# Edge beats paced by TensorE's traced pieces, and the last tile's output product moved into the second tile period

## The chip, the core and the metric

The kernel runs on one core of a Trainium2 chip. The metric is the device time of one execution in microseconds; three runs are shown for the kernel before. A core has TensorE (matrix products into PSUM), VectorE, ScalarE, GpSimd and SyncE, each working through its own queue in order. The profile writes PE, DVE, ACT, POOL and SP for them, and PEld for TensorE's weight loads. DMAs are issued from the queues of SP, ACT and POOL.

## The reference

625 nodes with 1024 features and 10000 directed edges go through two layers.

```
xn = layernorm(x)
x  = x + GAT(xn, edges) + linear_attention(xn)      # 4-head graph attention; 16 heads, phi = elu + 1
x  = x + bit_ffn(layernorm(x))                      # int8 activations, ternary weights
xn = layernorm(x)
x  = x + SAGE(xn, edges) + linear_attention(xn)
x  = x + attention_and_experts(x)                   # dense attention, 8 experts, 2 per token
```

The change lies in the first layer. Its graph attention computes for every edge, and for a loop at each node, `e = att . leaky_relu(xl[src] + xr[dst])` for four heads, takes the softmax over the edges that end in one node, and sums `xl[src]` with these weights. The result goes through `W_up`. The linear attention computes `q`, `k`, `v` by three 1024 x 1024 products, and its result goes through the output weights `Wo`. Both are added to `x`.

## The kernel before

The 625 nodes are five tiles of 125. The first part of the kernel, up to about 640 us, computes the whole first layer and begins the second. Its order is written out by hand: `do(prep, pe, after, after2)` (class `Stream`, L174) emits a piece of TensorE work, after emitting the drains (`after`) of the pieces before it. Each engine runs what was emitted for it, in that order.

**The edge stage.** The 10000 edges lie in 79 columns of up to 128. Column `t` needs two gathers from DRAM (`ga`, rows of `xl` by source; `gb`, rows of `xr` by destination, L591), a score on VectorE (L599, L571, L572, L574), an exponential on ScalarE (L578) and a scatter of four values into a table in DRAM (L609). Gathers and scatters are indirect DMAs issued by GpSimd, 237 in all. Columns go in groups of two (40 groups, the last with one short column); `ga` and `gb` have four buffers each. One *beat* `g` (`one_beat`, L662) emits the gathers of group `g`, the scores of group `g - 3`, the exponentials of `g - 4` and the scatters of `g - 5` (the list `lags`), and in beats 1 to 5 also the loop scores of one node tile. From the output products on, `lags` is 1, 1, 2, and a beat may emit four scatters.

Beats are laid between the pieces of the linear attention by an estimate: every piece calls `work(us)` with the time that it is held to take (L681), and a beat is emitted whenever the sum reaches 8.2 us times the number of beats so far. The pieces: for each half of the columns and each tile a `key` and a `value` product (20 in all) with up to six `count` pieces after each (79; L447, fed by one-hot tiles that VectorE writes up to eight ahead); eight `states`; eight `query` and eight `answer` pieces; then the output products `mixed(t)` with `Wo` (L717), 16 products of 512 columns each.

**The output products.** `mixed(0)` begins before the last answer with six of eight row blocks. Then come `mixed(3)` and `mixed(4)`, whose results VectorE drains with the bias into the tile `kept`; `weight_sums` (L740: absolute sums of the three FFN weight matrices on VectorE, L742), a small product `pm` with their means (L744), the rest of `mixed(0)`, `mixed(1)`, `mixed(2)`, and the rounding of the FFN weights to three values (`ternary`, L755). Tiles 0 to 2 stay in PSUM, which has three double banks for them. Beats that are left over are emitted after that.

**The tile periods.** `load_table(t)` (L803) fetches a tile of the table (`tb`), from GpSimd's queue. For each tile, `weigh` (L817) multiplies it with edge counts, `sums` makes the sums (`pg`) and `turn_sums` transposes them, `up_again` (L872) adds the product with `W_up` to the bank that holds `mixed(t)`, or for tiles 3 and 4 to a new bank, and adds that to `x` (L885). `x` itself is loaded again by GpSimd after the first table tile, and `bo` or `kept` is added to it (L1051). One period later the FFN of that tile follows (`ptr`, `pgu`, `phT`, `pdn`), and one later still its rows are transposed for layer 2. From period 2 on, `spacer()` puts the first `key` and `value` products of layer 2 between; their weights are asked for by `lin1.weights(0)`, and take the buffers of `Wo`.

Of the kernel before, what the change touches and what calls it, by code (L numbers as in the profile page):

```python
# [14 lines left out]
ALU = mybir.AluOpType  # L15
# [6 lines left out]
P = 125  # L22
# [8 lines left out]
KC = D // 128  # L31
# [22 lines left out]
def attempt(ctx: ExitStack, tc: tile.TileContext, w: dict, out: bass.AP, shifted: bool):  # L54

    nc = tc.nc
# [105 lines left out]
    def rows_dma(eng, dst, src):  # L162

        eng.dma_start(out=dst[0:112], in_=src[0:112])
        eng.dma_start(out=dst[112:P], in_=src[112:P])
# [42 lines left out]
    hold = {}  # L208

    def mid(shape, name):  # L210
        return midp.tile(shape, FP, tag="mid", name=name)
# [4 lines left out]
    class LinearAttention:  # L216
# [26 lines left out]
        def key(self, t):  # L243
            kf, bk, wk = self.kf, self.bk, self.wk

            def pe():
                hold["pk", t] = ps1("pk")
                group(hold["pk", t][:P], [(self.xnT[:, k, nodes(t)], wk(k)) for k in range(KC)])

            def after():  # L250
                kb = mix.tile([P, 512], FP, tag="kb", name="kb", bufs=1)
                nc.vector.tensor_tensor(kb, hold.pop(("pk", t))[:P], bk[:P], op=ALU.add)
                ke = mix.tile([P, 512], FP, tag="ke", name="ke", bufs=1)
                nc.scalar.activation(ke, kb, AF.Exp)
                nc.scalar.activation(kb, kb, AF.Relu)
                hold["k", t] = ke, kb

            def after2():
                ke, kb = hold.pop(("k", t))
                nc.vector.scalar_tensor_tensor(kf[:, t, :], ke, 1.0, kb, op0=ALU.min, op1=ALU.add)  # L260

            do(None, pe, after, after2)
            self.work(4.8)

        def value(self, t):
            v, bv, wv = self.v, self.bv, self.wv

            def pe():
                hold["pv", t] = ps1("pv")
                group(hold["pv", t][:P], [(self.xnT[:, k, nodes(t)], wv(k)) for k in range(KC)])  # L270

            def after():
                nc.vector.tensor_tensor(v[:, t, :, 0:128],
                                        hold.pop(("pv", t))[:P].rearrange("p (a b) -> p a b", a=4),
                                        bv[:P].rearrange("p (a b) -> p a b", a=4), op=ALU.add)

            do(None, pe, after)
            self.work(4.8)

        def states(self):  # L280

# [44 lines left out]
        def answer(self, m, oT):  # L326
            kv, a = self.kv[m // 4], m % 4

            def pe():
                hold["pdo"] = [feat("pd", [(kv[:, a, 128:256], hold["qf", m])]),  # L330
                               feat("po", [(kv[:, a, 0:128], hold["qf", m])])]

            def after():
                pd, po = hold["pdo"]
                z = mix.tile([128, NP], FP, tag="qe", name="z", bufs=1)
                nc.vector.tensor_scalar(halves(z), pd, 1e-6, None, op0=ALU.add)
                nc.vector.reciprocal(z, z)
                nc.vector.tensor_tensor(halves(oT[:, m, :]), po, halves(z), op=ALU.mult)

            do(None, pe, after)  # L340
            self.work(2.7)

    with ExitStack() as st0:
        main = st0.enter_context(tc.tile_pool(name="l0", bufs=1))
# [7 lines left out]
        with ExitStack() as edges:  # L352
# [327 lines left out]

            def work(us):  # L681
                beat["us"] += us
                while beat["us"] >= 8.2 * beat["g"] and chunks:
                    one_beat()

            work(0.0)
# [1 line left out]
            for c in range(2):  # L688
                if c:
                    lin.half(c)  # L690
                for t in range(NT):
                    for f in (lin.key, lin.value):
                        f(t)
                        part["held"] = max(part["held"] - 1, 0)
                        for _ in range(6):
                            if count():
                                work(0.72)
                states.append(lin.states())
                if c == 0:
                    for f in states[0]:  # L700
                        f()
# [12 lines left out]
                f()  # L714


            def mixed(t, ks=range(KC), keep=None):  # L717
                for c in range(2):
                    def pe(c=c):
                        if c == 0 and ks[0] == 0:  # L720
                            hold["px", t] = ps2("px1")
                        for k in ks:
                            nc.tensor.matmul(hold["px", t][:P, c, :], lhsT=oT[:, k, nodes(t)], rhs=wo[c](k),
                                             start=(k == 0), stop=(k == KC - 1 and keep is not None))

                    def after():
                        px = hold.pop(("px", t))
                        for c in range(2):
                            nc.vector.tensor_tensor(keep[:, c, :], px[:P, c, :], bo[c][:P], op=ALU.add)

                    do(None, pe, after if keep is not None and c == 1 else None)
                    work(0.6 * len(ks))

            dn = main.tile([128, 2, D], BF, name="dn")
            part3 = main.tile([128, 3], FP, name="part3")
# [43 lines left out]
            gu = wpool.tile([128, KC, 512], BF, tag="w", name="gu", padded_shape=[128, KC, 512])  # L779
            made = [gu[:, :, 0:256], gu[:, :, 256:512], dn]  # L780
            lags[:] = 1, 1, 2
            kept = mid([P, 2, 2, 512], "kept")
            mixed(3, keep=kept[:, 0])
            weight_sums()
            mixed(4, keep=kept[:, 1])
            weight_means()
            mixed(0, range(6, KC))
            for t in (1, 2):
                mixed(t)
                ternary(t)  # L790
# [9 lines left out]
        late = st0.enter_context(tc.tile_pool(name="l0r", bufs=1, reuse_waits="tile"))  # L800


        def load_table(t):  # L803

            hold["tb", t] = mid([P, NT, P, 4], "tb")
            if not shifted:
                rows_dma(nc.gpsimd, hold["tb", t].rearrange("p s d h -> p s (d h)"),
                         tview[:, :, t * 4 * P:(t + 1) * 4 * P])

        def weigh(t):  # L810
# [59 lines left out]
            do(None, pe, after)  # L870

        def up_again(t):  # L872
            kept_apart = t >= 3
            px = ps2("px1") if kept_apart else hold.pop(("px", t))

            def pe():
                goT = hold.pop(("goT", t))
                for c in range(2):
                    for k in range(2):
                        nc.tensor.matmul(px[:P, c, :], lhsT=goT[:, k, :],  # L880
                                         rhs=wu[:, k, c * 512:(c + 1) * 512],
                                         start=(kept_apart and k == 0), stop=(k == 1))

            def after():
                nc.vector.tensor_tensor(x[:, t, :].rearrange("p (c n) -> p c n", c=2), px[:P],  # L885
                                        x[:, t, :].rearrange("p (c n) -> p c n", c=2), op=ALU.add)

            do(None, pe, after)
# [116 lines left out]
            return p1, f1, f2, f3, f4, p5, f5  # L1005


        load_table(0)
        for t in range(NT):
            rows_dma(nc.gpsimd, x[:, t, :], xrows[t])  # L1010
        load_table(1)
# [4 lines left out]
        def spacer():  # L1016

            f, t = next(kv_pieces)
            getattr(lin1, f)(t)

        for p in range(NT + 2):
            do()
            if p >= 2:
                made_of[p - 2][5]()
            if 1 <= p <= NT:
                made_of[p - 1] = ffn(p - 1)
                made_of[p - 1][0]()
            if p >= 3:
                spacer()
            if p >= 2:  # L1030
                made_of[p - 2][6]()
            if p == 0:
                xnT1 = bigT("xnT1")
                nc.gpsimd.memset(xnT1[:, :, N:NP], 0.0)
                lin1 = LinearAttention(xnT1, ("L1_Wq", "L1_Wk", "L1_bk", "L1_Wv", "L1_bv"), w["L1_bq"],
                                       lambda us: None, nc.gpsimd)
            if p < NT:
                sums(p)
            if 1 <= p <= NT:
                made_of[p - 1][1]()  # L1040
                do()
                made_of[p - 1][2]()
            do()
            if p + 1 < NT:
                weigh(p + 1)
            if p + 2 < NT:
                load_table(p + 2)
            for t in ((0, 1), (2, 3, 4))[p] if p < 2 else ():
                for c in range(2):
                    xc = x[:, t, c * 512:(c + 1) * 512]  # L1050
                    nc.vector.tensor_tensor(xc, xc, bo[c][:P] if t < 3 else kept[:, t - 3, c, :], op=ALU.add)  # L1051
            if p == 0:
                lin1.weights(0)
            if p == 1:
                lin1.half(0, loaded=True)
            if 2 <= p <= NT:
                spacer()
            if p < NT:
                turn_sums(p)
            if 1 <= p <= NT:  # L1060
                made_of[p - 1][3]()
            do()
            if p < NT:
                up_again(p)
            if 1 <= p <= NT:
                made_of[p - 1][4]()
# [621 lines left out]
    for i in range(3):  # L1688
        d = 1 << i
# [240 lines left out]
```

## Time and profile before

| | us |
|---|---|
| median of three runs | 2255.76 (2247.72 to 2260.8) |
| the profiled execution | 2253.51 |
| its span in the trace | 2251.8 |
| TensorE busy | 2115.4 |
| VectorE busy | 715.1 |
| GpSimd busy | 341.6 |
| mean granted TensorE clock | 0.973 |

The span is what the trace covers; all sums below are made in it. The clock is the share of full speed that was granted to TensorE. Beginnings of stages in the trace: first key piece 49.0 us, first gather 56.3, end of the last output product 402.5, first product of the tile periods 456.3, layer 2's first key piece 524.1.

### The profile page before, as it was taken

To read this page: it belongs to the slowest core of one execution; us is meant where nothing else is said; L and a number is where in the kernel's file an instruction comes from. 1 tells how busy PE (TensorE), PEld (TensorE's weight loads), DVE (VectorE), ACT (ScalarE), POOL (GpSimd) and SP (SyncE) were. 2 spreads that over 40 slices of the span, in tenths; PEclk is the share of its full clock that TensorE was granted. 3 is DMA by queue.
4 is the path that set the end of the run, shared out by engine and by line. 5 is a ranking of instruction groups with operands and counts; after the bars stand their busy time and mean duration, and the time that the engine had idled before them with its cause. 6 is when DMAs were issued, how large, how long until landed. Compare 5 with 4: busy or idle time off the path is not lost. (4 is left out here: it accounts for less than half of the span.)

```text
span 2251.8 us, 17353 instructions
## 1 busy us (share of the span) xinstructions
PE 2115.4 (94%) x6934; PEld 1211.3 (54%) x6934; DVE 715.1 (32%) x1216; ACT 194.6 (9%) x354; POOL 341.6 (15%) x351
## 2 busy tenths in 40 slices
PE   7999999158899989999999999999999999999998
PEld 5665664035444658764445776556754444444443
DVE  4855486365621482001013233322111111111112
ACT  2101110001110110000000011110000000000000
POOL 1566477610000040010000000110000000000010
PEclk9999999668999999999999999999999999999999
DMA  8352332350030210231212111030288997898742
GB/s 278 118 165 70 136 127 55 120 135 23 19 103 29 84 56 1 75 116 61 75 38 103 38 38 38 19 102 7 87 313 323 332 331 283 321 332 303 262 149 94
DMA packets 145848, 301.62 MB, mean 134 GB/s; under 512 B 12370, under 2 KB 22436, under 8 KB 145754
## 3 DMA queue, kind: packets, MB, share of 16 engines
q1 hardware_dynamic: 123412, 243.18, 30.4%
q0 software_dynamic: 17664, 47.47, 7.1%
q10 hardware_dynamic: 4678, 9.72, 1.4%
q8 instruction: 58, 0.95, 0.2%
q14 instruction: 36, 0.29, 0.0%
HBM read 277.49 MB, written 22.84 MB: 133 GB/s over the span
## 5 line engine op out<-in xcount | busy, mean ns | idle before, releaser
L130 PE MATMUL pu<-w,xgT 128*128 128x512 f32 x768 | 333.9, 593 | 1.9 <-DVE xgT L1224 1.9
L130 PEld LDWEIGHTS pu<-w,xgT 128*128 128x128 f32 x768 | 144.0, 190 | 174.8 <-issue 172.0
L130 PE MATMUL pyb<-w,hb 128*128 128x512 f32 x384 | 174.3, 598 | 2.4 <-ACT yb L105 2.1
L130 PE MATMUL pv<-w,xnT 128*125 128x512 f32 x320 | 142.6, 599 | 4.7 <-DVE x L985 4.7
L130 PE MATMUL pk<-w,xnT 128*125 128x512 f32 x320 | 140.6, 592 | 0.0
L130 PE MATMUL pq<-xnT,w 128*128 128x313 f32 x512 | 138.1, 428 | 2.0 <-ACT qf L319 1.2
L130 PE MATMUL p<-tT,w 128*128 128x313 f32 x512 | 136.3, 428 | 0.4 <-DVE tT L1224 0.4
L130 PEld LDWEIGHTS pq<-xnT,w 128*128 128x128 f32 x512 | 96.5, 190 | 42.1 <-ACT qf L319 3.7
L130 PEld LDWEIGHTS pyb<-w,hb 128*128 128x128 f32 x384 | 69.8, 189 | 90.9 <-issue 74.8
L130 PEld LDWEIGHTS p<-tT,w 128*128 128x128 f32 x512 | 96.8, 190 | 37.9 <-issue 1.2
L1764 DVE TENSOR_TENSOR su<-pu,su 128x512 f32<-128x512 f32 x24 | 16.6, 692 | 314.2 <-ACT su L1763 314.2
L130 PEld LDWEIGHTS pv<-w,xnT 128*125 128x125 f32 x320 | 59.9, 190 | 78.9 <-issue 72.2
L130 PEld LDWEIGHTS pk<-w,xnT 128*125 128x125 f32 x320 | 59.6, 188 | 71.6 <-issue 70.7
L609 POOL DMA_INDIRECT table<-es,at x79 | 83.3, 1054 | 60.7 <-issue 32.8
L1747 POOL DMA_INDIRECT xg<-rows_d,slots x12 | 11.4, 947 | 524.7 <-PE pxg L1754 449.0
L591 POOL DMA_INDIRECT ga<-xl_d,si x79 | 79.9, 1012 | 62.7 <-DVE es L574 22.9
L130 PE MATMUL pg<-xl,pT 125*125 125x65 f32 x200 | 32.2, 332 | 57.5 <-DVE pT L817 55.4
L591 POOL DMA_INDIRECT gb<-xr_d,di x79 | 81.6, 1032 | 25.2 <-issue 25.2
L130 PE MATMUL px<-w,hT 128*125 128x512 f32 x160 | 70.3, 592 | 0.0
L130 PE MATMUL px<-w,oT 128*125 128x512 f32 x160 | 70.3, 592 | 0.0
L130 PE MATMUL ph<-meanT,w 128*128 128x313 f32 x256 | 70.1, 426 | 0.0
L130 PE MATMUL ph<-xnT,w 128*128 128x313 f32 x256 | 70.0, 427 | 0.0
(368 smaller groups left out, 2507.2 us busy)
## 6 DMA issues: line engine op xcount, KB each, us to landing
w<-in_eW_dram SPq DMA_DIRECT2D x144, 1024.0 KB
w<-in_L_Wk_dram SPq DMA_DIRECT2D x8, 1024.0 KB
w<-in_L_Wv_dram SPq DMA_DIRECT2D x8, 1024.0 KB
w<-in_L_Wq_dram SPq DMA_DIRECT2D x8, 1024.0 KB
w<-in_L_Wo_dram SPq DMA_DIRECT2D x8, 1024.0 KB
w<-in_W_self_dram SPq DMA_DIRECT2D x8, 1024.0 KB
w<-in_W_neigh_dram SPq DMA_DIRECT2D x8, 1024.0 KB
w<-in_sW_dram SPq DMA_DIRECT2D x8, 1024.0 KB
```

What stands on the lines that cost most here:

```text
L130: nc.tensor.matmul(dst, lhsT=lhsT, rhs=rhs, start=(i == 0), stop=(i == len(pairs) - 1))
L591: nc.gpsimd.indirect_dma_start(out=ab[g][side][0:p, j, :], out_offset=None, in_=src[:, :], in_offset=bass.IndirectOffsetOnAxis(ap=ix[0:p, ...
L609: nc.gpsimd.indirect_dma_start(out=table[:, :], out_offset=bass.IndirectOffsetOnAxis(ap=at[0:p, lo + j:lo + j + 1], axis=0), in_=es[0:p, l ...
L1747: nc.gpsimd.indirect_dma_start(out=xg, out_offset=None, in_=rows_d[:, :], in_offset=bass.IndirectOffsetOnAxis(ap=slots[:, b:b + 1], axis=0))
L1764: nc.vector.tensor_tensor(su, pu[:, 0, :], su, op=ALU.mult)
```

## The change

The estimates and due times of the beats are new, tile 4's output product is made in two halves in the second tile period, with layer 2's weights asked for after it, and the first table tile is loaded from ScalarE's queue.

```diff
 key, value:
-            self.work(4.8)
+            self.work(7.0)
 answer:
-            self.work(2.7)
+            self.work(2.3)
 one count:
-                                work(0.72)
+                                work(0.7)
 mixed, for each half:
-                    work(0.6 * len(ks))
+                    work(0.87 * len(ks))
 work:
-                while beat["us"] >= 8.2 * beat["g"] and chunks:
+                while beat["us"] >= 8.0 + 5.2 * min(beat["g"], 5) + 8.1 * max(beat["g"] - 5, 0) and chunks:
                     one_beat()

-            def mixed(t, ks=range(KC), keep=None):
-                for c in range(2):
+            def mixed(t, ks=range(KC), keep=None, cs=(0, 1)):
+                for c in cs:
...
-            kept = mid([P, 2, 2, 512], "kept")
-            mixed(3, keep=kept[:, 0])
+            kept = mid([P, 2, 512], "kept")
+            mixed(3, keep=kept)
             weight_sums()
-            mixed(4, keep=kept[:, 1])
+            mixed(0, range(6, KC))
             weight_means()
-            mixed(0, range(6, KC))
             for t in (1, 2):
                 mixed(t)
                 ternary(t)

-        def load_table(t):
+        def load_table(t, eng=nc.gpsimd):
...
-                rows_dma(nc.gpsimd, hold["tb", t]...
+                rows_dma(eng, hold["tb", t]...

 up_again:
-            kept_apart = t >= 3
+            kept_apart = t == 3

-        load_table(0)
+        load_table(0, nc.scalar)
         for t in range(NT):
             rows_dma(nc.gpsimd, x[:, t, :], xrows[t])
         load_table(1)
...
             if p >= 3:
                 spacer()
+            if p == 1:
+                mixed(4, cs=(0,))
...
-                    nc.vector.tensor_tensor(xc, xc, bo[c][:P] if t < 3 else kept[:, t - 3, c, :], op=ALU.add)
-            if p == 0:
+                    nc.vector.tensor_tensor(xc, xc, kept[:, c, :] if t == 3 else bo[c][:P], op=ALU.add)
+            if p == 1:
+                mixed(4, cs=(1,))
                 lin1.weights(0)
-            if p == 1:
                 lin1.half(0, loaded=True)
```

In the order of the changed kernel's instructions, TensorE's end of the edge stage reads: six blocks of tile 0, the last answer, tile 3, two blocks of tile 0, `pm`, tile 1, tile 2, and then the first `pg`. In the second period the first half of tile 4 stands between tile 0's up-product and tile 1's `pg`, the second half between tile 0's `pgu` and tile 1's transposes. All 43 beats come before the end of tile 2's product.

More of the change, by code (lines that the diff above doesn't have):

```diff
@@ L277, in value @@
             do(None, pe, after)
-            self.work(4.8)
+            self.work(7.0)
         def states(self):
@@ L800, in attempt @@
         late = st0.enter_context(tc.tile_pool(name="l0r", bufs=1, reuse_waits="tile"))
-        def load_table(t):
+        def load_table(t, eng=nc.gpsimd):
             hold["tb", t] = mid([P, NT, P, 4], "tb")
             if not shifted:
-                rows_dma(nc.gpsimd, hold["tb", t].rearrange("p s d h -> p s (d h)"),
+                rows_dma(eng, hold["tb", t].rearrange("p s d h -> p s (d h)"),
                          tview[:, :, t * 4 * P:(t + 1) * 4 * P])
```

## The prediction

> **What bounds the kernel now.** I read the slices first: TensorE is full everywhere except around 400 to 640 us. The stretches of that region, by engine (length, busy time and instruction count of PE, PEld, DVE, ACT, POOL, then granted clock, DMA share, GB/s):
>
> ```profile
> 375.00:402.50 27.50, 27.45 (x64) 11.66 (x63) 8.13 (x11) 0.42 (x2) 18.97 (x18) 1.00 0.42 137
> 402.50:445.20 42.70, 0.00 (x0) 0.00 (x0) 18.07 (x29) 1.04 (x5) 27.01 (x25) 0.56 0.24 77
> 445.20:456.30 11.10, 0.01 (x1) 0.01 (x1) 1.10 (x2) 0.00 (x0) 5.80 (x10) 0.50 0.73 174
> 456.30:480.00 23.70, 20.05 (x90) 15.68 (x90) 13.70 (x19) 1.66 (x2) 4.97 (x9) 0.67 0.73 185
> 510.00:524.00 14.00, 13.05 (x56) 11.59 (x57) 5.68 (x13) 2.47 (x4) 2.00 (x3) 0.52 0.20 51
> ```
>
> TensorE stands still for 54 us, and runs at half to two thirds of its clock for 70 us after. The timeline, engine by engine (start, duration, instruction, idle before it and releaser), says who holds it:
>
> ```profile
> 434.62 1.20 POOL L591 DMA_INDIRECT gb<-xr_d,di  x1 [0.30 <-issue]
> ...
> 444.27 0.85 POOL L609 DMA_INDIRECT table<-es,at  x1 [1.91 <-issue]
> 446.78 0.89 POOL L164 DMA_DIRECT2D tb<-table  x1 [1.66 <-issue]
> ...
> 456.29 0.68 PE L130 MATMUL pg<-xl,pT 125*125 125x65 f32 x2 [53.84 <-DVE pT L817]
> ```
>
> The last scatter of edge scores ends at 445.1; the table's first tile is fetched (446.8 to 455.2), VectorE multiplies it (1.05), TensorE starts: 11.2 us in all. So GpSimd's queue of 237 indirect DMAs is late, not TensorE. Who held that queue, from the waits up to 700 us (total, times, longest):
>
> ```profile
> POOL ga L591 <- DVE es L574: 22.9, 6, 7.3
> POOL table L609 <- DMA table<-es,at: 22.6, 11, 3.8
> POOL ga L591 <- DVE es L572: 13.9, 2, 10.2
> ```
>
> 37 us are gathers waiting for a buffer that VectorE has not scored yet; 23 us are scatters waiting for the scatter before. Without waits it paces itself: 276.10 to 331.39 holds 41 indirect DMAs, 1.35 us each, 8.1 us a beat of six. Last, what the weight statistics cost:
>
> ```profile
> 359.01 6.67 DVE L742 TENSOR_REDUCE part<-raw 128x1 f32<-128x2048 f32 x3
> ...
> 371.17 0.28 PE L130 MATMUL pm<-part,ones 128*128 128x3 f32 x2
> 371.31 31.14 PE L723 MATMUL px<-w,oT 128*125 128x512 f32 x72
> ```
>
> `pm` needs the three sums; they ended at 365.7, 5.5 us before TensorE came to it, because tile 4's product (13.8 us) lay between.
>
> **What the Trainium skill says.** "TensorE: Matmul & The Clock Gate", Part 1 and "Engine queue depths": about 3.4 us of dense work releases the clock, an idle window of that length halves it, and VectorE and ScalarE are strict first-in first-out. The trace agrees: 0.50 in the gap, 1.00 in dense stretches. The thin `pg` products did not release it (0.52 in the last row of the first view). "Trainium Kernel Development and Optimization", Key Constraints: queues of all engines share the same 16 DMA engines, a second issuer saves only issue time. I therefore price the table's new queue at the 1.66 us of POOL's wait plus some tenths of issue, not at a shorter transfer. "DMA: Bandwidth & Descriptors", Anatomy: about 2 us fixed, mostly the write's receipt. The scatters' median landing here is 2.1 us; in a row they start 2.4 to 2.9 us apart.
>
> **The change, part by part.** *Beats.* A beat issues two edge columns' gathers, the scores of an earlier group and older scatters. Old work estimates: 20 key/value pieces x 4.8, 79 counts x 0.72, 8 states x 0.6, 8 queries x 8.6, 8 answers x 2.7, five products x 9.6 = 296 us; at 8.2 a beat that is 37 beats (0 to 36) before the attention ends, the rest after it. TensorE really took 353 us (49.0 to 402.5). New: 20 x 7.0 + 55.3 + 4.8 + 68.8 + 18.4 + four products x 13.9 = 343; beat g falls due at 34 + 8.1(g-5), so all 43 do, the last at 334. The estimates now run at TensorE's own pace.
>
> The start: VectorE is full from 60 to 117 us. In the new order, three pairs of one-hots (0.57 a pair) and one key drain with its waits (3.3) come after group 0's scores instead of ahead: these start at 79, not 84.2. Beat 4 starts at 81 (86.6 before). Beat 6 waits for group 2's scores, which by the sum of VectorE's rows (one drain, five one-hot pairs, one self loop 3.1, one score 2.25) end at 97.5: it starts there (108.3). Two beats of 7.9: beat 8 at 113.4 (124.5). TensorE isn't touched: VectorE lags it by 10 us at most, three score banks and eight one-hots ahead cover that.
>
> From beat 8 to 37 no score is late: VectorE gets to them 10 to 20 us ahead of need, so the 22.9 us go. 180 DMAs x 1.35 = 243, and I keep the scatter waits, since the weight loads that go with them stay: 2.1 + 3.1 + 1.9 + 2.8 + 3.5 + 3.8 = 17. Beat 38 starts at 113.4 + 243 + 17 = 373.5.
>
> *Where the stall goes.* The lag falls from 3 to 1 at beat 38, now ahead of the sums: in the changed order VectorE does the scores of groups 35 to 38, then the sums, then tile 3's drain. Group 38's last gather is the seventh DMA of beat 38: 373.5 + 7 x 1.35 = 383, landed 2.8 later, 385.7; its score 2.25; the sums 6.67: 394.6. TensorE reaches `pm` at about 365 (13.8 us less product ahead, a few us of stall as VectorE waits for gathers) and stands there some 29 us; behind it in its queue are tiles 1 and 2's products, 27.7 us. With `pm` 0.3 and an estimated 1.7 for the cold clock (3.4 us at half, by the page) they end at 424.3. Beside that: the scatter tail (end of beat 38 at 384; four more in beat 39 and five, nine at about 2.45) ends at 406; the ternary rounding ends 13.5 after `pm`, at 408, and frees the table tile's buffer. Table: 408 + 8.4 + 1.05 = 417.5, perhaps 421 with the x rows now ahead of it. Both hidden by the products. On ScalarE's queue only tile 0's turned sums stand behind the load, and they need its result anyway. So the table's new queue is worth nothing here; without that cover its saving would be 2 us, or its loss 4.
>
> First `pg`: 424 against 456.3, **-32**.
>
> *Tile periods.* Tile 4's halves (6.9 each) enter the second. At full clock, by the rows of the fourth period, counted from the first `pg`: `pg` 4.6 (10.8 before), drain, turn, up-product to 10.3; VectorE's weighing and adds to 12.9, tile 0's add to 14.1, which frees the bank for tile 4. Its first half runs to 21.1, `pg` of tile 1 to 25.6 (before, done earlier: this is on the path, 6 us of VectorE idle). Turn, `pgu` to 30.1. Second half to 37.0: hidden, VectorE is weighing and adding until 42.5. Then two transposes, `pg` 4.6 (8.7 before), `pgu`: the first key piece of layer 1 starts at 59.3, against 524.05 - 456.29 = 67.8. Next period 0.9 shorter (34.0 for 34.9): **-9**. Layer 1's key weights may load only after the first half: 2 MB in a 25 us window with nothing else but a table tile. Dropping two drains of tile 4 (1.4 on VectorE) falls into its wait.
>
> Sum: -32 - 9 = **-41**. The profiled execution took 2253.51 (span 2251.8); that gives 2212. The median of the three runs is 2.2 higher: **2215**.
>
> Bounds of the unknown: scatter waits 0 to 25 (beat 38 at 356 to 382); the clock in the periods: half to full (+8 to -9).
>
> **Rivals.** (1) *No scatter waits*: `pm` 17 earlier, but the table, with tail and rounding, then allows no `pg` before about 408: -48 - 9, 2199. For: fewer loads in the tail (layer 1's weights, which ran at 402 to 420, move). Against: half of the waits lie before 275, beside loads that stay. (2) *Cold periods*: the 30 us stall at `pm` and gaps at the tile joints keep the clock near 0.6: -32 + 8, 2232. For: 0.52 at 510 to 524 though TensorE was 93% busy. Against: 27.7 us of dense products directly ahead, and 0.95 to 1.00 from 524 on, where 7 us pieces stand between. (3) *GpSimd gains nothing*, the slower side: removed waits come back as landing waits. In the old kernel group 38's gathers landed near 434; the same here puts `pm` at 443, the end of the products behind it at 473, 17 later than 456.3, and tile 4 in a half-clocked period takes the -9 away: 2273. It decides from a landing at 426 on, 40 us beyond my estimate, 1.47 instead of 1.35 us a DMA plus 18 more of waits. The change's aim, to finish with the attention, fails in all but (1).
>
> **How the numbers follow.** A measurement here can tell about 0.5% (11 us) from no change. Forecast 0.54 (2204 to 2226), (1) 0.18, (2) with a slower queue 0.18 (to 2244), (3) 0.10, half within 0.5% and half beyond. Faster 0.88, same 0.06, slower 0.06. Range 2195 to 2243: it leaves out 1 in 10 above and some of (1).
>
> **What would show it.** Right: TensorE idle 20 to 35 us ahead of `pm`, released by VectorE's sums, and almost none ahead of the first `pg`; GpSimd's waits for `es` under 15 us; last scatter near 406; clock 1.00 in the second tile period; VectorE idle some 6 us ahead of tile 1's drain. Wrong: first `pg` held by the table (rival 1, or x rows ahead of it), clock under 0.8 at 430 to 480 (2), last gather after 415 (3), or key weights late in the third period.

## The result and the profile after

The changed kernel takes 2238.95 us (median of five runs, 2236.13 to 2243.72), the kernel before 2255.76 beside it: a ratio of 0.9928, 95% interval 0.9900 to 0.9957. That is 17 us less where 41 were forecast; the direction and the range (2195 to 2243) held, the size did not. The profiled execution took 2242.49 us (span 2240.5).

The chain of work that the forecast followed is there, with other times. Timeline of the changed kernel (start, duration, engine, instruction, idle before it and releaser):

```profile
395.45 6.66 DVE L743 TENSOR_REDUCE part<-raw 128x1 f32<-128x2048 f32 x3
402.17 0.59 PE L130 MATMUL pm<-part,ones 128*128 128x3 f32 x2 [22.84 <-DVE part L743]
402.62 30.73 PE L724 MATMUL px<-w,oT 128*125 128x512 f32 x64
419.23 0.85 POOL L609 DMA_INDIRECT table<-es,at  x1 [1.90 <-issue]
421.19 0.33 ACTq L164 DMA_DIRECT2D tb<-table  x1
435.68 4.84 DVE L817 TENSOR_TENSOR pT<-tb,CT 125x500 f32<-125x500 f32 x5 [19.05 <-DMA tb<-table]
436.77 0.68 PE L130 MATMUL pg<-xl,pT 125*125 125x65 f32 x2 [3.42 <-DVE pT L817]
```

TensorE waits 22.8 us at `pm` for VectorE's sums, where some 29 were forecast. But the last scatter ends at 420.1, the table's first tile is multiplied only from 435.7 on, and the first `pg` follows the table, 3.4 us after the products have ended. It stands at 436.8: 19.5 us earlier than before (456.3), not 32.

The stretches between (length, busy time and count of PE, PEld, DVE, ACT, POOL, then granted clock, DMA share, GB/s):

```profile
379.30:402.20 22.90, 0.06 (x2) 0.04 (x1) 11.14 (x12) 0.42 (x2) 14.40 (x15) 0.55 0.13 37
402.60:433.40 30.80, 30.75 (x65) 12.97 (x65) 13.62 (x20) 0.20 (x1) 16.18 (x20) 0.90 0.41 103
433.40:436.70 3.30, 0.00 (x0) 0.00 (x0) 1.02 (x2) 0.00 (x0) 0.34 (x1) 0.90 1.05 262
436.70:456.00 19.30, 15.76 (x50) 11.13 (x50) 12.16 (x18) 1.66 (x2) 1.41 (x2) 0.58 0.45 120
456.00:480.00 24.00, 22.37 (x94) 13.10 (x95) 13.97 (x29) 3.19 (x5) 1.40 (x2) 1.00 0.61 185
480.00:505.50 25.50, 18.55 (x75) 14.35 (x75) 16.99 (x34) 2.95 (x6) 3.28 (x6) 0.67 0.27 85
```

In the third row the DMA engines are full while TensorE stands: that is the table's tile, with the `x` rows beside it. In the fourth row the clock is 0.58, and `pg` with its start takes 10.8 us as before: the gap, though short, was followed by the low clock. Only the stretch with tile 4's halves runs at full clock, and it falls again right after.

The waits, up to 700 us (total, times, longest):

```profile
POOL table L609 <- DMA table<-es,at: 23.8, 13, 3.7
POOL table L609 <- ACT es L578: 12.0, 2, 9.1
POOL ga L591 <- DVE es L572: 3.7, 1, 3.7
```

Of the 37 us in which gathers waited for scores, 3.7 are left. The scatters' waits for the scatter before stayed at 23.8, and a new one of 9.1 us stands at the first scatter.

One number orders all that follows: the time from the end of the last scatter to layer 2's first key piece. Before it was 78.9 us (445.1 to 524.1), now 85.4 (420.1 to 505.5); the code counts layers from 0, and the expectations below call it layer 1's. So the last scatter came 25 us earlier (39 by the forecast, 445 to 406), and what follows it took 6.5 us more than before. By the forecast it would have taken 77.3 us (406 to 483.3), 1.6 less than before.

### The profile page after: what moved, and what is told of

The parts are those of the page before. It is cut to its first block, busy times and chain, and to the rows that moved or that the text cites. A ratio compares the mean times of both kernels' runs of the same rounds, so it can differ in the third digit from the quotient of the medians.

```text
span 2240.5 us, 17360 instructions
## 1 busy us (share of the span) xinstructions
PE 2126.4 (95%) x6934; PEld 1217.3 (54%) x6934; DVE 714.2 (32%) x1214; ACT 194.8 (9%) x354; POOL 340.6 (15%) x349
## 5 line engine op out<-in xcount | busy, mean ns | idle before, releaser
L1766 DVE TENSOR_TENSOR su<-pu,su 128x512 f32<-128x512 f32 x24 | 16.6, 691 | 314.6 <-ACT su L1765 314.6
L130 PEld LDWEIGHTS pv<-w,xnT 128*125 128x125 f32 x320 | 59.6, 189 | 78.3 <-issue 71.6
L591 POOL DMA_INDIRECT gb<-xr_d,di x79 | 82.1, 1039 | 24.1 <-issue 23.8
L724 PE MATMUL px<-w,oT 128*125 128x512 f32 x160 | 74.5, 626 | 4.7 <-DVE z L336 2.9
L130 PE MATMUL px<-w,hT 128*125 128x512 f32 x160 | 70.3, 592 | 0.0
L130 PE MATMUL px<-w,oT 128*125 128x512 f32 x160 | 70.3, 592 | 0.0
```

The costliest lines, as they stand in the source:

```text
L130: nc.tensor.matmul(dst, lhsT=lhsT, rhs=rhs, start=(i == 0), stop=(i == len(pairs) - 1))
L591: nc.gpsimd.indirect_dma_start(out=ab[g][side][0:p, j, :], out_offset=None, in_=src[:, :], in_offset=bass.IndirectOffsetOnAxis(ap=ix[0:p, ...
L1766: nc.vector.tensor_tensor(su, pu[:, 0, :], su, op=ALU.mult)
```

## The experiments

Eighteen runs were made in five groups, each on one chip. The chips were of two kinds: on one, which had two groups, the kernel before took 2253 and 2255 us, as in the first measurement, and on three others 2275 to 2281. Below, "the faster chip" is the one, and "the slower chips" are the three. Ratios are to the kernel before on the same chip.

| kernel | before | this | ratio (95%) |
|---|---|---|---|
| after_again | 2253.03 | 2232.91 | 0.9912 (0.9891 to 0.9932) |
| loops_early | 2253.03 | 2230.24 | 0.9897 (0.9875 to 0.9918) |
| best_a | 2253.03 | 2224.71 | 0.9871 (0.9849 to 0.9893) |
| best_b | 2253.03 | 2216.51 | 0.9827 (0.9807 to 0.9847) |
| best_b2 | 2255.22 | 2216.41 | 0.9825 (0.9811 to 0.9838) |
| beats_only | 2280.97 | 2281.25 | 0.9994 (0.9976 to 1.0012) |
| move_only | 2280.97 | 2286.94 | 1.0024 (1.0005 to 1.0043) |
| old_queue | 2280.97 | 2281.85 | 1.0004 (0.9980 to 1.0028) |
| early_sums | 2280.97 | 2280.83 | 1.0001 (0.9980 to 1.0021) |
| beats_only2 | 2275.49 | 2279.23 | 1.0020 (1.0006 to 1.0034) |
| move_only2 | 2275.49 | 2282.52 | 1.0027 (1.0009 to 1.0045) |
| old_queue2 | 2275.49 | 2281.26 | 1.0027 (1.0012 to 1.0041) |
| sums_inside | 2275.49 | 2279.75 | 1.0012 (0.9996 to 1.0029) |
| after_third | 2278.55 | 2281.96 | 1.0013 (0.9988 to 1.0038) |
| beats_only3 | 2278.55 | 2284.32 | 1.0025 (1.0011 to 1.0038) |
| old_queue3 | 2278.55 | 2285.86 | 1.0032 (1.0016 to 1.0047) |
| sums_inside2 | 2278.55 | 2285.08 | 1.0019 (1.0001 to 1.0036) |

before_again, the kernel before, was run for its trace alone, 2256.07 us on the faster chip; on a slower chip there is no trace of the kernel before. The traces, in us: the end of the last scatter, from there to the first `pg`, from there to layer 2's first key piece, and the sum of the two.

| kernel | last scatter ends | to first `pg` | to first key | sum |
|---|---|---|---|---|
| before / before_again | 445.1 / 444.0 | 11.2 / 11.1 | 67.8 / 67.8 | 78.9 / 79.0 |
| after / after_again | 420.1 / 415.1 | 16.7 / 16.0 | 68.7 / 69.5 | 85.4 / 85.5 |
| loops_early | 412.4 | 16.2 | 70.4 | 86.6 |
| best_a | 404.6 | 18.1 | 67.2 | 85.3 |
| best_b / best_b2 | 409.1 / 408.9 | 18.0 / 17.5 | 60.1 / 59.6 | 78.1 / 77.1 |
| beats_only / 2 / 3 | 459.0 / 461.2 / 472.9 | 14.3 / 18.0 / 16.5 | 70.8 / 68.1 / 68.9 | 85.2 / 86.1 / 85.4 |
| move_only / 2 | 468.9 / 462.0 | 11.6 / 11.0 | 75.8 / 74.3 | 87.4 / 85.3 |
| old_queue / 2 / 3 | 471.5 / 465.0 / 471.6 | 12.9 / 12.1 / 12.9 | 75.6 / 74.9 / 74.5 | 88.6 / 87.0 / 87.4 |
| early_sums | 466.0 | 16.9 | 69.7 | 86.6 |
| after_third | 468.2 | 16.1 | 70.3 | 86.4 |
| sums_inside / 2 | 465.7 / 469.4 | 16.1 / 18.4 | 69.2 / 70.4 | 85.3 / 88.8 |

### The parts alone

The first group took the change apart.

```diff
 beats_only = before, with the new estimates and due times only
-            self.work(4.8)
+            self.work(7.0)
...
-                while beat["us"] >= 8.2 * beat["g"] and chunks:
+                while beat["us"] >= 8.0 + 5.2 * min(beat["g"], 5) + 8.1 * max(beat["g"] - 5, 0) and chunks:
 move_only = after, with the old estimates and the table on GpSimd's queue
 old_queue = after, with
-        load_table(0, nc.scalar)
+        load_table(0)
 early_sums = after, with
+            weight_sums()
             lags[:] = 1, 1, 2
...
             mixed(3, keep=kept)
-            weight_sums()
```

> The kernel before with the beats' new estimates alone: tile 4's product stays ahead of the weight sums' reader, the table is fetched by GpSimd's queue ahead of the x rows. My theory: GpSimd's indirect DMAs end where they do in the changed kernel (near 420 us), TensorE waits some 12 us at `pm` (not 23, since 10 us more of products lie ahead of it), its products end near 435, the table is there by 431, so the first `pg` follows with no idle ahead of it, near 435, at the full clock (4.6 us instead of 10.8), and the first layer-1 key piece near 497 (505.5 in the changed kernel). Time 2225 to 2237, so the beats are the whole gain and tile 4's move is a loss of 2 to 10. Rival: the parts add up as forecast, the move is worth 9, and this one is slower than the changed kernel, 2245 to 2250.

> The changed kernel with the old beats and the table's first tile on GpSimd's queue: of the change only tile 4's halves in the second tile period (with layer-1's weight load behind them). My theory: GpSimd ends near 445 and the first `pg` stands at 456 as before; the 13.8 us taken from ahead of `pm` come out of a wait, and one half (7 us at full clock, 11 at the cold one) is now on the path of the second period: 2256 to 2266, slower than before by 0 to 0.5%. Rival (the forecast's step): the second period runs at full clock and gives 9 back: 2247.

> The changed kernel with the table's first tile again on GpSimd's queue, ahead of the x rows. My theory: the landing takes 8 to 9.5 us instead of 12.8, since the x rows no longer go ahead; the table is multiplied by 431 and the first `pg` follows the products (433.4) with no idle; without the gap of 3.4 us the clock stays up and `pg` takes 4.6 us instead of 10.8: 7 to 9 us less than the changed kernel, 2230 to 2233. Rival 1: the clock drops all the same, only the 3.4 us of idle are gained, 2235. Rival 2: the landing is slow for another reason (the table was just written) and nothing changes, 2239.

> The changed kernel with VectorE's three weight sums moved ahead of the last answer's drain, so that they no longer stand behind the scores of the last edge groups. My theory: TensorE's wait of 22.8 us at `pm` falls to nothing or a few us, some 6.7 us of wait appear ahead of tile 3's product instead, the products end near 415 instead of 433; GpSimd's tail and the table decide, and the first `pg` moves by 0 to 3 us (the ternary rounding no longer runs beside the last scatters): 2235 to 2240, with TensorE idle for 15 to 20 us ahead of the first `pg`. Rival: the wait at `pm` is what the change lost, and without it the first `pg` comes 10 us or more earlier: 2228 or less.

All four came out at the time of the kernel before or a little above it, on a chip where that one took 2281 us. None of the times that I had written down was met, and the ratios can't be set beside 0.9928. The traces show that TensorE itself was late there (more on that below). Two further groups fell on such chips again; the comparison is therefore made with after_third, the changed kernel on one of them. The steps after the last scatter can be read in the traces all the same. early_sums went the way that was expected, by less: no wait at `pm`, 5.7 us ahead of tile 3's product, and 7.5 us ahead of the first `pg`, where 15 to 20 had been written down.

> The changed kernel itself once more, beside the others, since the first four runs fell on a chip where the kernel before takes 2281 us instead of 2256. My theory: where TensorE issues without holes it is 0.7% below the kernel before (ratio 0.993); on a chip where it issues slowly in places, the drains and scores queued behind it on VectorE come late and the gathers wait for them again, so that the gain of the beats is gone (ratio 0.998 to 1.002). Rival: the change is worth the same 0.7% on any chip.

> beats_only once more, for a chip on which TensorE issues without holes (the kernel before at about 2253 us). My theory: `pm` where it is in the changed kernel (397), after a wait of some 12 us instead of 22.8; products of 31 us behind it end near 430; the table, first on GpSimd's queue, is there by then; `pg` at 430 at the full clock, but the second table tile comes late behind the x rows, as in best_a, so the first layer-1 key piece is near 497 (500.6 in the changed kernel): 2228 to 2234, ratio 0.989 to 0.992, so tile 4's move and the table's queue bring nothing together or cost a few us. Rival (the forecast's sum): without the move the periods are 9 us longer, 2242, ratio 0.995.

> move_only once more, for such a chip. My theory: GpSimd still decides (first `pg` near 456), the first period stays cold since TensorE stood for 50 us ahead of it, one half of tile 4 is on the path (7 us and more) and shortens nothing: equal to the kernel before or up to 0.4% slower, ratio 1.000 to 1.004. Rival (the forecast's step): full clock in the second period and 9 us gained, ratio 0.996.

> old_queue once more, for such a chip. My theory: the table's first tile is multiplied from 425 on instead of 430, the products (to 427) decide the first `pg`: 4 us earlier than in the changed kernel, and with a shorter gap ahead the clock drops later or not at all, for up to 5 us more: 4 to 9 us less than the changed kernel, ratio 0.987 to 0.9895. Rival: the 4 us are lost again when the second table tile waits behind the x rows; ratio 0.991 as the changed kernel.

> The changed kernel itself, as the measure for the three beside it. My theory: ratio 0.991 to 0.993 where TensorE issues without holes (the kernel before near 2253 us). Where the kernel before takes 2275 or more, the holes in TensorE's issue make the gathers wait for scores again and the ratio is 1.000 to 1.003, as those of its variants were there. Rival: the ratio is near 0.992 on such a chip too, and the variants lost there what they changed.

> beats_only beside the changed kernel. My theory: within 5 us of the changed kernel on the same chip, to either side: tile 4's move with the table's queue is worth nothing or less, for the full clock that it was to bring is not there. Rival (the forecast's sum): 9 us slower than the changed kernel.

> old_queue beside the changed kernel. My theory: where TensorE issues without holes the table's first tile is there 5 us earlier and the first `pg` follows the products, 4 us earlier; less than the changed kernel by 2 to 9 us. Rival: the 4 us are lost again when the second table tile waits behind the x rows; equal.

The changed kernel repeats its gain on the faster chip (after_again, 0.9912) and has none on a slower one (after_third, 1.0013), as the expectation of after_again said.

**With the old beats the move is a loss.** move_only is slower than the kernel before both times (1.0024, 1.0027, both intervals above 1), on slower chips. From the last scatter to the first key it takes 87.4 and 85.3 us, against 78.9 in the kernel before on the faster chip (the changed kernel takes 85.4 and 85.5 on that chip and 86.4 on a slower one, so the chip is worth about 1). The trace shows one half of tile 4 on the path at a low clock, after a wait for tile 0's add. Timeline of move_only2:

```profile
473.09 0.68 PE L130 MATMUL pg<-xl,pT 125*125 125x65 f32 x2 [52.88 <-DVE pT L817]
...
496.34 8.54 PE L724 MATMUL px<-w,oT 128*125 128x512 f32 x16 [5.17 <-DVE x L885]
...
531.04 1.93 PE L1000 MATMUL ptr<-ident,xn 125*128 125x125 f32 x8 [4.24 <-DVE xn L992]
533.73 8.66 PE L130 MATMUL pg<-xl,pT 125*125 125x65 f32 x40 [0.77 <-ACT xnT L1001]
...
574.54 4.58 PE L130 MATMUL pg<-xl,pT 125*125 125x65 f32 x40 [0.68 <-ACT xnT L1001]
```

The third `pg` takes 8.66 us here too, as in all 20 traces; dense pieces 20 us earlier do not keep the clock up to it. In all of them TensorE stands 3.4 to 4.2 us for VectorE's `xn`, just ahead of the transposes that come before this `pg`. The fourth `pg`, with no such wait, takes 4.58 us in 15 traces and 7.8 to 8.0 in five, so a wait of that length isn't the only thing that goes with the low clock. Whether the move costs or gains once the new beats are there can't be told: beats_only3 and after_third differ by 0.1%, within their intervals.

**On the slower chips the table's queue brings nothing, and costs nothing in the end.** The wait from the last scatter's end to VectorE's product with the table is 9.9 to 11.1 us where GpSimd's queue loads the tile ahead of the `x` rows (before, best_a, and all of move_only, beats_only and old_queue) and 14.9 to 17.3 where ScalarE's queue loads it beside them (after, its two repeats, loops_early, early_sums, sums_inside). "Trainium Kernel Development and Optimization", Key Constraints, says that all queues share the same 16 DMA engines; the trace agrees, with a DMA share of 1.05 in the gap ahead of the first `pg`. But the 3 to 4 us by which old_queue's first `pg` is earlier are lost one tile later. Timeline of old_queue3:

```profile
484.49 0.84 PE L130 MATMUL pg<-xl,pT 125*125 125x65 f32 x6
...
499.35 4.82 DVE L817 TENSOR_TENSOR pT<-tb,CT 125x500 f32<-125x500 f32 x5 [7.97 <-DMA tb<-table]
...
506.48 1.23 DVE L885 TENSOR_TENSOR x<-px,x 125x1024 f32<-125x1024 f32 x1
507.76 8.71 PE L724 MATMUL px<-w,oT 128*125 128x512 f32 x16 [11.67 <-DVE x L885]
```

Now the second table tile stands behind the `x` rows. VectorE waits for it, in order, and tile 0's add, which frees the bank for tile 4's half, comes behind. TensorE waits 11.67 us. The rival of old_queue2 was right: a transfer that is put first makes the next one last. On the faster chip old_queue was not run.

**On the slower chips `pm`'s wait costs nothing by itself.** sums_inside puts the sums where VectorE is free and TensorE has 14 us of product to do.

```diff
-            mixed(3, keep=kept)
-            weight_sums()
+            mixed(3, keep=kept, then=weight_sums)
 in mixed, behind do(...):
+                    if c == 0 and then:
+                        then()
```

> The changed kernel with the three weight sums inside tile 3's product, behind the last answer's drain and ahead of the scores that wait for gathers; nothing else. My theory: TensorE's wait of 22.8 us at `pm` is gone, the products end near 402 instead of 427, and TensorE stands some 25 us ahead of the first `pg` instead, since the table (issued when the last scatter has landed) decides: first `pg` 0 to 4 us earlier, ratio 0.989 to 0.9915. Rival: `pm`'s wait is what keeps the gain small; first `pg` 10 us or more earlier, ratio 0.987 or less.

> sums_inside beside the changed kernel. My theory: where TensorE issues without holes its wait of 22.8 us at `pm` is gone and stands ahead of the first `pg` instead, for the table decides; 0 to 4 us less than the changed kernel. Rival: 10 us less or more.

The first `pg` of sums_inside2 and of after_third, by their timelines:

```profile
442.93 0.28 PE L130 MATMUL pm<-part,ones 128*128 128x3 f32 x2
...
487.79 0.68 PE L130 MATMUL pg<-xl,pT 125*125 125x65 f32 x2 [17.00 <-DVE pT L818]
```

```profile
450.23 0.59 PE L130 MATMUL pm<-part,ones 128*128 128x3 f32 x2 [10.00 <-DVE part L743]
...
484.30 0.43 PE L130 MATMUL pg<-xl,pT 125*125 125x65 f32 x2 [3.69 <-DVE pT L817]
```

The wait at `pm` is gone and stands ahead of `pg`: 17.0 us instead of 3.7. The time (1.0019) is that of after_third (1.0013) within the intervals. In after_third `pm`'s wait was 10 us; that the 22.8 us of the faster chip move in the same way is not measured alone, only within best_a.

### The start

after_again and loops_early ran on the faster chip.

```diff
-                if 1 <= g <= NT:
-                    self_loops(g - 1)
+                for t in {1: (0,), 2: (1,), 3: (2,), 4: (3, 4)}.get(g, ()):
+                    self_loops(t)
```

> The changed kernel with the self loops of tiles 3 and 4 both at the fourth beat, so that the fifth loop's write to the table no longer lies ahead of the first scatter. My theory: the first scatter's wait of 9.1 us shrinks to under 4, beat 6 starts 5 to 7 us earlier, and as the pace after it is the same, so do the last gather, `pm` and the last scatter, and the end: 5 to 7 us less than the changed kernel. Rival: the scatter waits for the group's own scores and exponentials; then nothing moves by more than 2 us.

The first scatter, by the timelines of after_again and of loops_early:

```profile
96.22 1.00 POOL L609 DMA_INDIRECT table<-es,at  x1 [9.31 <-ACT es L578]
```

```profile
90.44 1.24 POOL L609 DMA_INDIRECT table<-es,at  x1 [0.31 <-ACT es L578]
```

The scatter waited for the fifth loop's write to the same table (its DMA was issued 1.0 us after that loop's exponential, at 95.1 in the changed kernel, some 3.7 us ahead of the scatter). With that loop one beat earlier the wait is 0.3 us, and beat 6 starts at 96.1 instead of 101.8. The group's own exponential, which the rival named, had ended 13.8 us ahead of the scatter in after_again. So the cause is right. The gain isn't: of these 5.7 us 2.8 are left at the last gather and 2.6 at the first `pg`, and the two times (2230.2 and 2232.9) can't be told apart. Most of the rest was lost by 180 us, where weights are loaded. The waits on GpSimd's queue of loops_early at 144 to 187 us, and of after_again over the same gathers, at 151 to 190:

```profile
POOL table L609 <- DMA table<-es,at: 8.4, 4, 3.7
POOL table L609 <- issue: 4.3, 5, 3.1
```

```profile
POOL table L609 <- DMA table<-es,at: 5.9, 2, 4.1
POOL table L609 <- issue: 2.1, 7, 0.3
```

GpSimd comes to this stretch 7 us earlier, but the weight loads don't: SyncE issues those at 138.0 to 161.2 us of after_again at 142.7 to 165.9 here. They follow TensorE, which with two loops in one beat waits 3.5 us for VectorE's one-hot tiles up to 180 us (0.6 in after_again). More scatters land beside them: the median landing is 4.1 us in that stretch, 2.1 in after_again's.

### A kernel that beats both

best_a is beats_only with loops_early's and sums_inside's edits and shorter lags for the last beats; best_b also moves the `x` rows. Both stand for all their edits together; what each is worth on this base was not measured alone.

```diff
 best_a:
                 elif m == 5:
+                    lags[:] = 2, 2, 3
 best_b:
-            rows_dma(nc.gpsimd, x[:, t, :], xrows[t])
+            rows_dma(nc.sync, x[:, t, :], xrows[t])
```

> The new beats without tile 4's move, with three edits: the loops as in loops_early; the three weight sums behind the last answer's drain and ahead of the beats' scores, inside tile 3's product; lags of 2, 2, 3 groups from the sixth answer on, so that half of the eight scatters that ran alone at the end go between gathers. The table's first tile is on GpSimd's queue ahead of the x rows. My theory: no wait at `pm`, products end near 421 (on the faster chip), GpSimd's tail ends 8 to 14 us earlier than in the changed kernel, table there by 419, first `pg` near 421 with no idle and at the full clock; then the second table tile, which waits behind the x rows, is the next thing late (some 5 us). 12 to 18 us less than the changed kernel on the same chip. Rival: lag 2 makes VectorE wait for gathers ahead of the answers' drains, TensorE stalls for as much as the tail gains, and it is equal to beats_only.

> best_a with the five x rows on SyncE's queue instead of GpSimd's. My theory: they are fetched before the table's first tile is due, so the second table tile no longer shares the DMA engines with 2.5 MB of them: the second `pg` comes 4 to 8 us earlier, 3 to 8 us less than best_a. Rival: their memory comes free no earlier, so they still run beside the table's tiles, and it is within 2 us of best_a or slower.

best_a is 8 us under the changed kernel, where 12 to 18 were written down. Its last scatter ends at 404.6 (415.1 in after_again): four scatters run alone at the end instead of eight. Its first `pg` is where I put it, 422.7, with no idle ahead and at 4.48 us, but its timeline goes on:

```profile
422.69 4.48 PE L130 MATMUL pg<-xl,pT 125*125 125x65 f32 x40
...
438.46 0.65 PE L130 MATMUL pg<-xl,pT 125*125 125x65 f32 x2 [5.71 <-DVE pT L820]
```

The second table tile is late by 5.7 us, and the clock falls. The rival's part is real too: with the lag of 2, TensorE waits 7.5 us ahead of tile 0's product. best_b takes 8 us more off; its timeline:

```profile
427.14 4.48 PE L130 MATMUL pg<-xl,pT 125*125 125x65 f32 x40
...
440.00 4.48 PE L130 MATMUL pg<-xl,pT 125*125 125x65 f32 x40
```

Both `pg` take 4.48 us, 12.9 us apart instead of 15.8. My reason for it was wrong, though: the `x` rows are not fetched ahead of the table. SyncE issues them at 414.9, beside it (issued at 410.9). What changed is the second table tile, issued at 413.0 instead of 420.4, since ten `x` DMAs no longer stand ahead of it in GpSimd's queue. From the last scatter to the first key best_b takes 78 us, and its repeat 77.

> best_b once more, for the chip of this call. My theory: on a chip without holes 0.983 again; on one with holes its shorter tail, earlier loops and x rows still count though the beats do not, ratio 0.990 to 0.997. Rival: with holes nothing of it is left, 1.000 or more.

> The kernel before itself, for a trace of it on the chip of this call. My theory: on a chip where it takes 2275 us or more, its trace too shows holes in TensorE's issue, but fewer than the changed kernel's on such a chip (24 us of idle put down to issue between 130 and 330 us there against none on a chip without holes), and GpSimd's gathers wait some 70 us for VectorE's scores instead of 37; first `pg` some 20 us later than 456. Rival: its attention stage runs as on the other chips, and only the later stages are slower.

best_b2 repeats it: 0.9825. It ran on the faster chip, which has no such holes (next section), so whether best_b wins on the other kind is open. before_again, on the same chip, could not show the kernel before there; it shows the trace of the first measurement once more (first `pg` at 455.1).

### Why nothing was won on the other chips

Busy times and clocks from 130 to 330 us (columns as above), first of after_again:

```profile
130.00:330.00 200.00, 192.15 (x737) 123.12 (x736) 123.28 (x213) 23.34 (x57) 142.59 (x141) 0.98 0.42 132
```

Then of after_third, with TensorE's longest group of waits in that stretch:

```profile
130.00:330.00 200.00, 158.56 (x562) 92.34 (x562) 85.09 (x186) 14.94 (x42) 122.86 (x123) 0.86 0.32 99
```

```profile
PE pct L447 <- issue: 21.0, 22, 2.4
```

And of move_only2, with the old beats on such a chip:

```profile
130.00:330.00 200.00, 188.20 (x697) 116.12 (x695) 108.22 (x195) 19.31 (x48) 116.24 (x116) 0.97 0.37 122
```

```profile
PE pct L447 <- issue: 6.0, 10, 1.7
```

On the slower chips TensorE stands between single matmuls with nothing that the trace shows to wait for, in stretches of some 20 us. From 60 to 400 us these holes sum to 23 to 44 us in the ten runs with the new beats, to 8 and 15 in the two with the old ones, and to none in any kernel on the faster chip. VectorE's drains queue behind TensorE and its edge scores behind the drains, so the gathers wait for scores again: 62.2 us in after_third, 5.2 in after_again. The forecast's premise, that the estimates now run at TensorE's pace, holds only where TensorE keeps the traced pace. The whole difference lies in this stage: after_third's last scatter ends 53.1 us later than after_again's, and its span is 53.9 us longer. What makes the holes, and why the new beats have more of them, stays open.

## Where the prediction failed, and where it held

**Pace and stalls.** Beat 4 at 81: it started at 81.6. From beat 8 to beat 38, 260 us forecast: 261 measured. The 22.9 us of gathers waiting are gone, the scatter waits stayed, as taken (16.6 us between these beats for 17); rival (1) needed them gone. Rival (3), removed waits coming back as landing waits, did not come there: the last gather was issued at 395.9, not after 415.

One term failed without cost: TensorE was to reach `pm` at about 365, after "a few us of stall", and reached it at 379.3. VectorE, with more scores ahead of its drains, holds it for 8.9 us at the first query product (0.8 before), which then takes 10.99 us instead of 8.69, and for 2.9 us more ahead of tile 3's. As `pm` waits for the sums in any case, this only made the wait there shorter: 22.8 us for 29.

**The step that failed first** is "Beat 6 waits for group 2's scores". It summed VectorE's rows and left out GpSimd's own queue: the first scatter stands ahead of beat 6 and waits for the loops' writes to the same table. Beat 6 started at 104.6, not 97.5. The trace of before had shown such a wait (5.79 us ahead of its first scatter, at 103.1). Everything behind it is 7 to 9 us late: beat 38 (382.0 for 373.5), the sums, `pm` (402.2 for 394.6). loops_early showed the wait's cause, and that taking it away gives back 2.6 us at the first `pg`.

**The step that failed at the end** is the tail "at about 2.45" a scatter and the table at 8.4, "both hidden by the products". The scatters ended at 420.1, not 406: 8.5 us from the late start of beat 38, the rest mostly from the scatters themselves. Eight ran alone, 2.9 us each on the mean (397.0 to 420.1), and three of them took 2.37, 2.31 and 1.83 us instead of 0.96 while VectorE rounded the weights (404.9 to 416.1). In the kernel before, too, the two indirect DMAs beside this rounding took 1.97 and 2.22 us. The table's tile then took 14.5 us from issue to VectorE's product; the forecast had named the `x` rows ahead of it and priced them at 4. So the table, not the products, came last, by 3.4 us. Products: 31.2 us with `pm` for 29.7. Of the 12.5 us that the first `pg` is late, 7.6 stand ahead of `pm`, 1.5 in the products and 3.4 in the gap: -19.5 for -32. That the table takes 3 to 4 us less when it is loaded first is measured (old_queue), though on the slower chips alone.

**The tile periods** were to give 9 and gave none: 68.7 us to the first key against a forecast of 59.3. The step that failed is "at full clock", and two terms are the difference: the first `pg` with its start at 10.8 us and the third at 8.66, both taken as 4.6. For the third the forecast gave no reason; the wait for `xn` that stands ahead of it (3.43 us before, 4.24 after) was in the trace of before. The second period's clock of 1.00, VectorE's idle of 6.1 us ahead of tile 1's drain and the hidden second half were as forecast. For the first `pg`, "at full clock" rested on no gap ahead of it; "TensorE: Matmul & The Clock Gate", Part 1, says that an idle window of about 3.4 us takes the clock back, and the trace agrees: 3.42 us of idle, then 0.58. In the 11 traces in which TensorE stood 3.4 us or more ahead of the first `pg`, it ran at half clock; of the nine without a gap, eight had it at full clock (4.48 us in best_a). The ninth is old_queue: 32 of its matmuls took 6.91 us, with no wait over 0.52 us ahead, so the rule doesn't tell all. Rival (2), 2232 to 2244, had a low clock in the periods from the stall at `pm` and from gaps between tiles, and the result lies in its span. The stall was made good by the products (clock 1.00 from 425 us on); the gaps were not. But the second period ran at full clock against it, and the late table is not in it, so that its number fits is in part luck.

**The rest.** The forecast had named a first `pg` held by the table, with the `x` rows ahead of it, as a sign of being wrong, and this sign came. The late first scatter is not among the unknowns that it named, so that the result still lies in its range is in part luck. By the two traces 18.5 us are won at the first key piece, and 11.3 at the end of the span: in the profiled execution the fourth period ran at a clock of 0.79 (539 to 580 us) and lost 7. after_again's periods there take 34.9 and 34.0 us, as before, so this belongs to that execution.

## What to carry to other kernels

When a queue is relieved, follow it to its end, and look for the first instruction on it that waits for a write to the same memory, by whatever queue it was made. A transfer that is moved ahead, or to another queue, makes another one last: write down for each what waits behind it one tile later. And pacing laid out by one trace's durations is worth what that trace's pace is worth; on a chip where TensorE ran slower, the same edit was worth nothing.

## What was not expected of the hardware

- Chips differ by 1%: the kernel before took 2253 and 2255 us on one, and 2275, 2279 and 2281 on three; the ratio of the changed kernel was 0.991 on the first and 1.001 on the one of the three where it ran.
- TensorE's holes on these three: one `pct` matmul every 0.7 to 2.8 us, over some 20 us, with no cause that the traces show.
- A scatter's time on GpSimd rose from 0.96 to as much as 2.37 us while VectorE rounded weights. "SBUF — State Buffer", SBUF: two separate sides, says that VectorE in a faster mode locks GpSimd out of the port with which it writes descriptors; the trace fits that, but no run here took the rounding away.
